# Scatters without a chain, layer 0's experts in two sets of sorted tokens, layer 1's tile weights by ScalarE's queue and its gate rows through DRAM

## The chip, the cores and the metric

The kernel runs on one core of a Trainium2 chip. The time is the device time of one execution in microseconds (us); of several runs the median is taken. Engines are named as the profile names them: PE (TensorE; PEld is its weight load), DVE (VectorE), ACT (ScalarE), POOL (GpSimd), SP (SyncE, which only issues DMAs). A queue is the row of DMAs that one of SP, ACT and POOL issues in its own order of instructions.

## The reference

Two transformer layers on x of 8 batches x 256 tokens x 128 channels, in float32. Every layer modulates with six vectors for each batch, made from a condition c:

```python
mod = (_silu(L0_c) @ L0_wmod).reshape(L0_c.shape[0], 6, 1, -1)
sa, ca, ga, sb, cb, gb = (mod[:, 0], mod[:, 1], mod[:, 2], mod[:, 3], mod[:, 4], mod[:, 5])
...
h = _layernorm(x, axis=-1) * (1 + ca) + sa
x = x + ga * _L0_attn_ref(h, ...)
h = _layernorm(x, axis=-1) * (1 + cb) + sb
x = x + gb * _L0_ffn_ref(h, ...)
```

Layer 1 has the same form with its own parts. Both attentions are causal with 16 heads, of 8 channels in layer 0 and of 64 in layer 1. Layer 0's FFN is a shared expert (128 to 512 to 128, GELU) plus the best 2 of 8 experts of that size for each token, weighted by the router's softmax, divided by the sum of the two. Layer 1's FFN is the token itself, a shared gated expert (128 to 64 to 128, SiLU) and the best 2 of 16 such experts, weighted by a sigmoid router's two values, divided by their sum.

## The kernel before

**Tiling.** The 2048 tokens are 8 batches, 4 windows of 512 (two batches each) and 16 token tiles of 128. The residual x stays in SBUF, one tensor for each window. Transposed, modulated activations h (channels on the partitions) feed the matmuls.

**Order.** The program is written in units, but a scheduler puts each engine's instructions in their final order when the kernel is built, by the tiles that they read and write and by its own estimates of time. So the order of one engine is fixed before the run, and an instruction waits for everything that stands ahead of it on its engine. Tiles come from pools with a fixed number of buffers; a new tile waits until the buffer's earlier user is done. PSUM is used by four names: ps_a with 3 buffers, ps_b with 2, ps_c and the fourth with 1.

**Attention** of both layers runs through `pipelined`: for each unit (a batch and a group of heads) scores, exp on ACT, causal select on POOL (L788), values, and between them `also0` or `also1`, which take one step of a list of further work (layer norms, routing, combining) at each call.

**Sorted experts.** The class `Sorted` (z0, L992, for layer 0 and z1, L993, for layer 1's windows 0 to 2) sends each token to its two experts. `place` finds each token's row within its expert's region (matmul rk, L870; counts pre and seen on POOL, L867) and scatters the rows of one window by 8 indirect DMAs on POOL (L882; one 128-token tile and one choice each, 64 KB) into a DRAM tensor xs that has been cleared. All write to the same tensor, so each waits until the one before has landed. `tables`, called once all windows are placed, makes from the counts the rows and the expert of each tile beyond the first 128 tokens of an expert, and where each token's results will lie (cnt, then some 30 small DVE operations). `load_rows` (L967) loads a tile's 128 rows through SP with a row number read from a register, `load_weights` (L971) its weights through POOL by an indirect DMA (514 KB for layer 0, 128 KB for layer 1), `gather` (L979) brings 128 tokens' results back from the DRAM tensor ys, two indirect DMAs on POOL for each token tile.

**Layer 0's FFN** has 39 tiles: 8 first ones with resident weights wst, then up to 31 more. For each: transpose xT (L1226), hidden hp and GELU hst, projection yt (L1247), a copy to ysb, a store to ys by SP (L1252). Before the tiles stand the last window's routing and, between its parts, the shared expert over the 4 windows (hp L1177, ysh L1190, and the gates' transpose gp with its copy gT, which multiplies the experts' biases). Layer 1 begins with the gathers (L979) of batches 0 to 3, each window's combine (L1347), layer norm 1a (xn1a L739, transposes nt1a L748) and the projections.

**Layer 1's FFN** has 40 tiles in 10 groups of 4 for windows 0 to 2, 16 first ones and 24 more; each group's results leave by one store from ACT's queue, after one copy on DVE and one on ACT (L1582). The last window is not sorted: it runs over 8 pairs of experts and the shared one (g L1596, u L1598, a, of L1617), and its gates are spread over each pair's 128 rows by a copy gm on POOL (L1605) and four transposes gp on PE (L1608), read from PSUM in

```python
nc.vector.tensor_tensor(a, a, gp.rearrange("p a m -> p (a m)"), ALU.mult)
```

(L1609). Then come the gathers of windows 0 to 2, tc (L1643, L1646), the additions to x, and the output's DMAs.

## Time and profile before

| | us |
|---|---|
| median of 3 runs | 710.91 (707.64 to 711.27) |
| profiled execution | 704.31 |
| its span | 702.6 |
| last batch of layer 0's attention (y) ends | 153.8 |
| first expert tile of layer 0 | 206.1 |
| last yt of layer 0 | 286.7 |
| first matmul of layer 1 (nt1a) | 312.9 |
| last y of layer 1's attention | 591.5 |
| last tile group of layer 1 | 637.1 |
| last gather issued | 675.1 |
| last addition ends, then only the output's DMA | 690.7 |

How to read it: the profile is one execution. Each engine's busy time comes first, then the span in 40 slices of 17.6 us with a digit for the busy tenths. Waits are listed as "who, for whom: us in total, times, longest us". "PEclk" is the clock granted to PE, in tenths of full speed. An "issue" wait is time without a recorded cause. A DMA's price has two parts: the time its issue takes on the queue, and the time until it lands (scatter 0.98 and 2.3 us in the median, xg 0.33 and 3.4, ys by SP 0.33 and 2.9, ys by ACT 2.3 to land).

### The profile page before, as it was taken

To read this page: it belongs to the slowest core of one execution; us is meant where nothing else is said; L and a number is where in the kernel's file an instruction comes from. 1 tells how busy PE (TensorE), PEld (TensorE's weight loads), DVE (VectorE), ACT (ScalarE), POOL (GpSimd) and SP (SyncE) were. 2 spreads that over 40 slices of the span, in tenths; PEclk is the share of its full clock that TensorE was granted. 3 is DMA by queue.
4 is the path that set the end of the run, shared out by engine and by line. 5 is a ranking of instruction groups with operands and counts; after the bars stand their busy time and mean duration, and the time that the engine had idled before them with its cause. 6 is when DMAs were issued, how large, how long until landed. Compare 5 with 4: busy or idle time off the path is not lost. (4 is left out here: it accounts for less than half of the span.)

```text
span 702.6 us, 12856 instructions
## 1 busy us (share of the span) xinstructions
PE 583.3 (83%) x4927; PEld 409.7 (58%) x4927; DVE 338.8 (48%) x994; ACT 245.9 (35%) x435; POOL 341.3 (49%) x493
## 2 busy tenths in 40 slices
PE   3898877866969999319999999999989987889672
PEld 3455443433859999316666666667667756654451
DVE  5358566574412222253146345743554585833561
ACT  2546262615125555204433443344323521222110
POOL 6667457744540444475223332247234754864840
PEclk9999899988989999859999999999999999889886
DMA  8899930011253999221011202030203022662220
GB/s 278 313 407 398 375 139 13 21 51 77 80 189 120 292 331 322 63 52 35 2 43 31 65 1 62 1 77 17 62 8 77 10 68 69 183 199 72 60 57 20
DMA packets 48291, 83.30 MB, mean 119 GB/s; under 512 B 6253, under 2 KB 26765, under 8 KB 47069
## 3 DMA queue, kind: packets, MB, share of 16 engines
q1 hardware_dynamic: 33388, 51.84, 22.6%
q0 software_dynamic: 9552, 27.93, 12.8%
q10 hardware_dynamic: 5280, 2.62, 1.3%
q8 instruction: 41, 0.67, 0.4%
q14 instruction: 30, 0.24, 0.1%
HBM read 51.33 MB, written 31.04 MB: 117 GB/s over the span
## 5 line engine op out<-in xcount | busy, mean ns | idle before, releaser
L788 POOL TENSOR_SCALAR_AFFINE_SELECT pt<-pt 128x256 f32<-128x256 f32 (+1 forms) x176 | 90.8, 545 | 117.6 <-ACT pt L1390 104.5
L882 POOL DMA_INDIRECT xs<-ht,idx x56 | 59.4, 1061 | 79.4 <-DMA xs<-ht,idx 65.3
L971 POOL DMA_INDIRECT wt<-in_wpk_dram,widx x55 | 52.6, 956 | 63.3 <-PE xT L1226 50.7
L1390 ACT ACTIVATE pt<-sc 128x768 f32<-128x768 f32 x64 | 48.9, 808 | 88.2 <-PE sc L1387 88.0
L979 POOL DMA_INDIRECT yg<-ys,yidx x56 | 54.0, 965 | 33.5 <-issue 21.9
L1094 ACT ACTIVATE pt<-sc 128x1024 f32<-128x1024 f32 x48 | 46.8, 1021 | 59.7 <-PE sc L1090 58.6
L1407 PE MATMUL o<-pt,v 128*64 128x256 f32 (+1 forms) x512 | 57.1, 337 | 0.0
L1407 PEld LDWEIGHTS o<-pt,v 128*64 128x64 f32 x512 | 34.1, 137 | 32.1 <-issue 14.7
L1387 PE MATMUL sc<-q,k 64*128 64x256 f32 (+1 forms) x512 | 50.9, 338 | 0.0
L1387 PEld LDWEIGHTS sc<-q,k 64*128 64x128 f32 x512 | 41.8, 188 | 10.3 <-issue 5.9
L1238 ACT ACTIVATE hst<-hp,wt 128x128 f32<-128x128 f32 x124 | 35.4, 368 | 26.8 <-ACT hst L1238 17.7
L592 DVE COPY k<-kp 128x512 f32<-128x512 f32 x29 | 20.0, 689 | 43.8 <-PE kp L1363 41.6
L1251 DVE COPY ysb<-yt 128x128 f32<-128x128 f32 x39 | 11.4, 291 | 56.5 <-PE yt L1247 50.9
L1115 PE MATMUL o<-pt,vm 128*32 128x128 f32 (+1 forms) x512 | 32.3, 350 | 6.9 <-POOL pt L788 6.9
L1363 PE MATMUL qp<-h,wq 128*128 128x256 f32 x128 | 36.8, 410 | 0.8 <-DVE h L752 0.8
L1370 PE MATMUL vp<-wv,h 128*128 128x512 f32 x64 | 35.2, 631 | 1.9 <-DVE k L592 1.6
L1090 PE MATMUL sc<-qm,k 32*128 32x512 f32 x192 | 34.0, 646 | 1.0 <-ACT pt L1094 0.9
L1236 PE MATMUL hp<-xTs,wt 128*128 128x128 f32 x248 | 33.5, 278 | 1.5 <-DMA wt<-in_wpk_dram,widx 0.9
L1363 PE MATMUL kp<-h,wk 128*128 128x256 f32 x128 | 34.3, 392 | 0.0
L592 DVE COPY ou<-o 128x512 f32<-128x512 f32 x29 | 19.9, 686 | 28.0 <-PE o L1407 28.0
L1247 PE MATMUL yt<-wt,hst 128*128 128x128 f32 x248 | 32.6, 275 | 0.0
L1236 PEld LDWEIGHTS hp<-xTs,wt 128*128 128x128 f32 x248 | 30.1, 191 | 3.3 <-issue 1.5
(284 smaller groups left out, 1147.8 us busy)
## 6 DMA issues: line engine op xcount, KB each, us to landing
xs<-zero SPq DMA_DIRECT2D x1, 12288.0 KB
xs<-zero SPq DMA_DIRECT2D x1, 8192.0 KB
rb<-rd SPq DMA_DIRECT2D x14, 512.0 KB, 6.2
wst<-in_wpk_dram SPq DMA_DIRECT2D x8, 514.0 KB, 42.5
mdb<-mrd SPq DMA_DIRECT2D x2, 2048.0 KB
xg<-xs SPq DMA_DIRECT2D x63, 64.0 KB, 3.4
ys<-ysb ACTq DMA_DIRECT2D x10, 256.0 KB, 2.3
ys<-ysb SPq DMA_DIRECT2D x39, 64.0 KB, 2.9
```

The lines of the kernel that those rows point to most:

```text
L592: nc.vector.tensor_copy(dst, src)
L788: nc.gpsimd.affine_select(out=pt, in_=pt, compare_op=ALU.is_ge, fill=0.0, base=0, pattern=[[0, pt.shape[1]], [1, P]], channel_multiplier=-1,)
L882: nc.gpsimd.indirect_dma_start(out=self.xs[:, :], out_offset=bass.IndirectOffsetOnAxis(ap=idx[:, j, k : k + 1], axis=0), in_=tokens[:, j, ...
L971: nc.gpsimd.indirect_dma_start(out=wt, out_offset=None, in_=packed, in_offset=bass.IndirectOffsetOnAxis(ap=self.widx[:, d : d + 1], axis=0),)
L979: nc.gpsimd.indirect_dma_start(out=yg[:, k, :], out_offset=None, in_=self.ys[:, :], in_offset=bass.IndirectOffsetOnAxis(ap=self.yidx[:, j, ...
L1094: nc.scalar.activation(pt[:, bass.ts(half, 2), :], sc, AF.Exp)
L1236: nc.tensor.matmul(out=hp[:, c, :], lhsT=wt[:, bass.ts(c, P)], rhs=xT, start=True, stop=True)
L1238: nc.scalar.activation(hs[:, c, :], hp[:, c, :], AF.Gelu_apprx_tanh, bias=wt[:, WB + c : WB + c + 1])
L1363: nc.tensor.matmul(out=ps_[:, n, :], lhsT=w1[f"w{what}1"][:, bass.ts(2 * part + n, P)], rhs=hb, start=True, stop=True,)
L1387: nc.tensor.matmul(out=sc[:, n, cols], lhsT=k[r, c, bass.ts(kb, P)], rhs=q[r, c, qs], start=True, stop=True)
L1390: nc.scalar.activation(pt, sc[:, :, 0:384], AF.Exp, scale=1.0 / math.sqrt(D1))
L1407: nc.tensor.matmul(out=o[bass.ts(n, D1), m, qs], lhsT=v[:, kb, bass.ts(4 * u + 2 * m + n, D1)], rhs=pts[m][:, n, cols], start=(kb == 0), s ...
```

## The change

1. The scatters of one set are declared free of each other (`apart`): each waits for the clearing only; the last of a set waits for all others, and stands for them towards the reader of xs. This is in the class, so it holds for both layers.
2. Layer 0's tokens are two sets: windows 0 to 2 (31 tiles) and window 3 (15 tiles), 46 tiles in place of 39, with two tensors xs (6 and 2 MB) in place of one (8 MB). The first set's tables are made at the end of the attention. Its tiles are written ahead of the shared expert of windows 1 to 3, which now stands between the sets. The gathers of batches 0 to 3, their combine and layer norm 1a of windows 0 and 1 are called beside the second set's tiles; 16 gathers are left to layer 1.
3. `also0` and `also1` take two steps at a call.
4. Layer 1's extra tiles get their weights by a plain DMA on ACT's queue, from an expert number read into a register of ACT. The groups' second copy goes from ACT to DVE, the stores from ACT's queue to SP's.
5. The last window's gates are transposed once (4 transposes, one copy), stored to DRAM (gd) and read back broadcast over 64 partitions by 4 DMAs of SP into gp in SBUF. `gate_rows()` is called ahead of the first tile group. The copies gm and the 32 transposes are gone.
6. Buffers: hs has one buffer, sums1 is gone (r tiles and r_last), hgb is xn itself; mdb1 keeps its place in the program, but its pool opens after the tiles of both sets.

```diff
+    def apart(self, ins):
+        group = f"scatters{self.tag}"
+        if len(self.scatters) + 1 < 2 * self.ng * self.nt:
+            if self.scatters:
+                tc.declare_no_dep(ins, group=group, reason="different rows")
+                tc.add_manual_dep(ins, self.fill.name, WAIT, reason="rows are cleared first")
+        else:
+            for other in self.scatters:
+                tc.add_manual_dep(ins, other.name, WAIT, reason="stands for all scatters")
+        tc.add_to_no_dep_group(group, ins)
+        self.scatters.append(ins)
...
-    z0 = Sorted(xp, "0", E0, NW, TT, (2 * NT - 2) // P)
+    zs0 = [Sorted(xp, f"0{n}", E0, k, TT, (2 * k * TW - 2) // P) for n, k in enumerate((NW - 1, 1))]
...
         def also0(n):
-            if st0["steps"]:
-                st0["steps"].pop(0)()
+            for step in st0["steps"][:2]:
+                step()
+            del st0["steps"][:2]
...
                     st0["steps"].append(lambda w=w: route0(w, ps_ln))
+                    if w == NW - 2:
+                        st0["steps"].append(lambda: zs0[0].tables(ps_ln, True))
...
-        last = layernorm_steps(NW - 1, md[0], SB, CB, f"0b{NW - 1}", ps_b, make_tokens0)
-        last[0]()
-        hs = shared_hidden(0)
-        last[1]()
+        for step in layernorm_steps(NW - 1, md[0], SB, CB, f"0b{NW - 1}", ps_b, make_tokens0):
+            step()
         route0(NW - 1, ps_b)
-        shared_project(0, hs)
-        z0.tables(ps_b)
+        zs0[1].tables(ps_b, True)
...
+        tiles = [(z, n) for z in zs0 for n in range(E0 + z.nd)]
+        first = E0 + zs0[0].nd
+        shared_project(0, shared_hidden(0))
         for n in range(3):
-            fetch(n)
-        for w in range(1, NW):
-            hs = shared_hidden(w)
-            shared_project(w, hs)
...
+            if n == first:
+                for w in range(1, NW):
+                    shared_project(w, shared_hidden(w))
+            if first < n <= first + 4:
+                gather(n - first - 1, fp0)
+            if n == first + 4:
+                combine(0, fp0)
+                combine(1, fp0)
+                steps = layernorm_steps(0, md[1], SA, CA, "1a0", ps_b)
+                steps.pop(0)()
+            if n == first + 6:
+                steps.pop(0)()
+            if n == first + 8:
+                combine(2, fp0)
+                combine(3, fp0)
+                steps = layernorm_steps(1, md[1], SA, CA, "1a1", ps_b)
+                steps.pop(0)()
+            if n == first + 10:
+                steps.pop(0)()
...
-        for b in range(4):
-            gather(b)
-        for step in after0(0):
-            step()
...
-                    z1.load_weights(wt[:, t, :], i["wpk1"], d)
+                    r = nc.values_load(
+                        z1.widx[0:1, d : d + 1], engines=[mybir.EngineType.Activation], min_val=0,
+                        max_val=(E1 - 1) * P, skip_runtime_bounds_check_because="an expert's number, 128 times",
+                    )
+                    nc.scalar.dma_start(out=wt[:, t, :], in_=i["wpk1"][bass.ds(r, P), :])
...
-            nc.scalar.copy(ysb[:, :, 1, :], y[1])
-            nc.scalar.dma_start(
+            nc.vector.tensor_copy(ysb[:, :, 1, :], y[1])
+            nc.sync.dma_start(
...
+        gp = fp1.tile([P, NP, TW], F32, bufs=1, name="gp")
+        def gate_rows():
+            gT_ps = ps_b([E1, TT, P], "gT1")
+            for j in range(TT):
+                nc.tensor.transpose(gT_ps[:, j, :], gates1[:, j, :], ident)
+            gT = fp1.tile([E1, TT, P], F32, bufs=1, name="gTs1")
+            nc.vector.tensor_copy(gT, gT_ps)
+            gd = dram.tile([NP, 2, TW], F32, name="gd1")
+            nc.sync.dma_start(
+                out=gd.rearrange("p n q -> (p n) q"), in_=gT.rearrange("e j t -> e (j t)")
+            )
+            for half in range(2):
+                p = bass.ts(half, NP // 2)
+                for n in range(2):
+                    nc.sync.dma_start(out=gp[bass.ts(n, I1), p, :], in_=gd[p, n, :].partition_broadcast(I1))
...
             if p < NP:
-                gm = fp1.tile([P, TT, 2, I1], F32, tag="gm", bufs=2, name=f"gm1_{w}_{p}")
-                src = gates1[:, :, 2 * p : 2 * p + 2]
-                nc.gpsimd.tensor_copy(gm, src.unsqueeze(3).to_broadcast([P, TT, 2, I1]))
-                gp = ps_b([P, TT, P], f"gp1_{w}_{p}")
-                for j in range(TT):
-                    nc.tensor.transpose(gp[:, j, :], gm[:, j].rearrange("p a m -> p (a m)"), ident)
-                nc.vector.tensor_tensor(a, a, gp.rearrange("p a m -> p (a m)"), ALU.mult)
+                nc.vector.tensor_tensor(a, a, gp[:, p, :], ALU.mult)
...
+        gate_rows()
         for m in range(3):
             fetch1(m)
         turn1(0)
```

## The prediction

> **What bounds the kernel now.** I read the busy table and the 40 slices first, then the waits, then a table of stages. PE is busy 83% of the span, and in slices 12 to 29 it reads 9: layer 1's attention, which the change hardly touches. What can move lies in the other slices.
>
> ```profile
> PE 583.3 (83%) x4927; PEld 409.7 (58%) x4927; DVE 338.8 (48%) x994; ACT 245.9 (35%) x435; POOL 341.3 (49%) x493
> PE   3898877866969999319999999999989987889672
> PEclk9999899988989999859999999999999999889886
> ```
>
> The stages (start:end, length, then busy us of PE, PEld, DVE, ACT, POOL) show where PE is not busy.
>
> ```profile
> 30.00:154.00 124.00, 102.32 (x1318) 57.52 (x1310) 80.54 (x253) 50.55 (x56) 80.38 (x116) 0.94 0.55 209
> 154.00:206.00 52.00, 39.76 (x211) 28.25 (x211) 18.78 (x74) 17.32 (x23) 27.38 (x30) 0.87 0.32 102
> 206.00:287.00 81.00, 78.57 (x663) 75.88 (x663) 19.52 (x78) 45.42 (x157) 24.42 (x26) 0.98 0.79 257
> 287.00:315.00 28.00, 1.28 (x5) 0.86 (x5) 11.52 (x48) 0.70 (x2) 20.53 (x21) 0.58 0.18 47
> 315.00:590.00 275.00, 264.22 (x2171) 183.58 (x2172) 136.90 (x319) 103.78 (x149) 109.55 (x190) 0.99 0.16 37
> 590.00:640.00 50.00, 40.35 (x326) 28.50 (x324) 27.08 (x63) 11.58 (x26) 30.93 (x32) 0.86 0.60 172
> 640.00:702.60 62.60, 39.49 (x160) 23.46 (x158) 29.06 (x55) 5.96 (x10) 30.17 (x32) 0.80 0.16 44
> ```
>
> PE idles 22 us in layer 0's attention, 12 in its routing, 27 between the layers, 11 in layer 1's attention, 33 in the last two stages, 12 of which are the output's DMA after the last addition. The waits (who, for whom, total us, times, longest) say for what.
>
> ```profile
> POOL xs L882 <- DMA xs<-ht,idx: 65.3, 38, 5.1
> PE nt1a L748 <- DVE xn1a L739: 26.3, 1, 26.3
> POOL yg L979 <- issue: 21.9, 51, 8.1
> PEld o L1115 <- POOL pt L788: 10.2, 8, 3.7
> PE rk L870 <- DVE m L862: 8.8, 6, 2.5
> ```
>
> L882 is the chained scatters; behind them on POOL stand the causal selects (L788) that layer 0's values wait for. The 26.3 is one wait: the last expert tile is stored, 12 to 13 gathers must land, window 0 is combined and normalized, and only then has PE layer 1's first matmul. The end is a chain of gathers: after the tiles (yq_9 ends at 637.1) the first of 24 gathers issues at 640.9, the last lands at 677.6, the last window's output is added by 690.7.
>
> ```profile
> POOL yg L979 2%; PE of L1617 1%; DMA yg<-ys,yidx 1%; PE g L1596 1%; PE u L1598 1%; POOL x L1625 0%; DVE a L1609 0%; PE gp L1608 0%; POOL wt L971 0%; DVE tf L1623 0%; DVE tc L1646 0%; DVE x L1627 0%; POOL gm L1605 0%; DVE tc L1643 0%; DVE x L1647 0%
> ```
>
> **What the skill says.** "DMA: Bandwidth & Descriptors", the section on the anatomy of a GpSimd-path DMA: about 2.0 us fixed, most of it the receipt of the last write, plus bytes over 436 GB/s; 64 KB gives 2.15 us. The trace agrees: a scatter issues in 0.98 us and lands 2.3 us later, so a chained one costs 3.3 us and more, an unchained one its issue. Same page, "Issuing engines are not separate DMA queues": another queue saves sequencer time only, so layer 1's weight loads on ACT's queue free POOL and buy no bandwidth. No run here shows that yet. Same page, "Two DMAs through the same engine are not ordered": the second must wait for the first's semaphore, so gate rows through DRAM cost two landings in turn. "TensorE: Matmul & The Clock Gate", Part 1: an idle window of some 3.4 us halves PE's clock. Here PE's granted clock is 0.58 between the layers and 0.87 in the routing stage; after stalls of even 2 us matmuls took twice their time for about 2 us.
>
> **The change, part by part.** Times are on the profiled execution (704.31 us, span 702.6), which lies 6.6 us under the median of 710.91; I carry the difference over.
>
> *A. Scatters apart, layer 0's attention.* Eight scatters take 8 x 1.25 = 10 us (issue 0.98 plus about 0.3 to the next) instead of 8 x 3.3 to 5. In the changed order they sit where PE has 13 us of other work before it needs the next select. The stalls on selects of 1.14, 2.15 and 3.24 us go; of the rank waits about half of 8.8, and one to two us of half-clock work after each. Gain 9 (bounds 3 and 12). Against it: window 0 to 2's table (some 30 small DVE operations of 0.3, 9 us) now stands on DVE ahead of the last batch's reciprocal; I take 1.5 (0 to 4). Layer 0's attention ends at about 146 instead of 153.75: -7.5.
>
> *B. Tiles before window 3 is routed.* Before, 206.06 - 153.75 = 52 us lie between, of which shared windows 1 to 3 took 25 as cover, 4.03 were a wait for a POOL operation behind scatters and 6.00 a wait for xg behind 48 us of scatters. Now the router of window 3 has no shared window beside it (6.5 us of PE idle, at nothing before because hidden), but the 10 us of waits go: tiles start 25 us after attention, 171.
>
> *C. Set 1* is 31 tiles, not 39: the first 8 took 17.3 us, the others 2.04 each: 17.3 + 23 x 2.04 = 64. End 235.
>
> *D. Between the sets* the moved shared windows (25 us) should hide the gathers. But the static order of DVE puts the copy gT_2 behind the combine of gather 13, and gT_3 behind gather 15 and window 0's normalization; PE has the transposes of tiles 2 to 4 of set 2 behind these copies, as two PSUM buffers serve both. The gathers start when ys_30 has landed (235 + 0.3 + 2.9), gather n lands 1.25(n-1) + 2.6 later, with one 1.27 us addition between: the 15th 21 us after the start, at 260, gT_3 at 261.5. PE has 13.5 us of work and is there at 248.5. New stall: 13 (6 if the gathers start earlier than I think, 14 at most), with PE cold behind it, 1 us. Then 11.5 us of shared work and 15 tiles (27 us, 1.8 each, most from resident weights): layer 1's first matmul at about 301.5, not 314.87. The 7 extra tiles are in this: 13 us of PE, and 7 x 642 KB beside it.
>
> *E. Into layer 1.* Before, the first select was at 331.04 and the first value matmul at 337.0. Now 16 gathers (20 us) stand on POOL between the last store's landing (about 303) and the first select: select at 326, values at 328. PE has 22 us of projections and scores, which fill 301.5 to 324. Gain -9. In the same attention scatters and selects meet again. Windows 0 and 1's blocks have 20 us of cover; window 2's last seven (9 to 11 us) stand before a select for which PE has 6.2 us of work: stall 4 (0 to 5). Attention ends at about 586.5, not 591.5: -5.
>
> *F. Last stage.* Taken away: 24 weight issues on POOL (0.96 each, beside other work), 8 gm copies (5 us among the gathers), 32 transposes (8.7 us) on PE. Added: 24 loads on ACT, each with a register load like xg's on SP (0.94 us per load there). Two of these come ahead of the last rstd1b and seven ahead of the routing exp, which on the clock of before starts at 603.6 instead of 598.2 (bounds of the delay 0 and 9). PE has the gate transpose gT ahead of the first tile's; it needs the whole routing chain on DVE (ready at 613.3 before, with POOL's loads beside it; now about 608 on that clock), so tiles begin at 609 instead of 597.7. Loads run ahead meanwhile, so groups then go at PE's pace (31.7 us busy) and at SP's, which carries gd, four gp reads and the ys stores as well: last group 644 instead of 637.1, first gather +6.6. Given back: the gm copies, the gate transposes, and fewer products left behind the last gather, -5. Sum +1.5 (bounds -3 and +7).
>
> Stores by SP instead of ACT: 0.33 against 0.4 us of issue, landing 2.9 against 2.3; no more than 0.6, at the last group only. The second ysb copy on DVE, hgb in xn, r in tiles: no cover lost, nothing. mdb1's 2 MB now stands in SP's queue ahead of set 2's first store; it waits for gT_3 at latest, which is over by then.
>
> *Sum.* Entry of layer 1 -9, window 2's block +4, last stage +1.5: -3.5. So 700.8 for the profiled execution, 707.5 on the median's scale: -0.5%, just what a measurement of this kernel can tell from no change.
>
> **The rivals.** *Faster by much*: the copies in D are not late (the gathers overtake PE's work, or PE's 25 us really cover them) and F's gT costs little since weights bound that stage. Then D gives back 10, F 2 and the block 2: 707.5 - 14 = about 693, and up to 702 if a third comes true. For it: the slices show 54 us of poor PE use between 154 and 315 that the shared windows could fill. Against: the static order of DVE names the gathers ahead of the copies.
>
> *Slower*: head of line in the last stage. PE's gT ahead of xT_0 turns ACT's late exp into a wait of the whole tile stage. From the point where the loads behind it no longer catch up (exp over 6 us late), the 24 gathers, which are the tail chain, start that much later: +10 there, and A worth only 3 (+6): 707.5 + 13 to 16, about 721. For it: ACT has no 3 us of slack between rstd1b at 593.2 and the exp at 598.2. Against: PE had 6 us of idle in 598 to 636 that absorb part.
>
> *No effect*: since the gathers before layer 1's first select stay 16 in number, E's gate on POOL could eat all: +4, 711. It is counted in the middle case.
>
> **Chances.** Middle (702 to 714, forecast 707.5): 0.42. Faster rival (692 to 702): 0.28. Slower rival (714 to 728): 0.30. Four fifths lie in 694 to 722. Faster by over 0.5% (below 707.4): 0.28 + 0.19 = 0.47; within 0.5% (to 714.5): 0.23; slower: 0.30.
>
> **What would show it.** A: waits of scatters on scatters vanish, PE's wait for pt L788 under 3 us, attention ends at 146 to 150. B, C: first xT near 171, last yt of set 1 near 235. D: one PE wait of over 8 us at the transposes of set 2, released by DVE. E: select near 326, values near 328. F: a PE wait of some 11 us for gT, with ACT's loads ahead of the exp; last tile group near 639. Wrong would make me: no wait in D (then faster), a long wait for xg behind the chain to DRAM in F, or set 1 slowed by the second clearing's and shared weights' traffic.

## The result and the profile after

The changed kernel takes 734.61 us in the median (731.78 to 737.06, 4 runs) against 710.7 us (707.64 to 711.27, 4 runs): 1.034 times as long [1.030, 1.039]. Forecast were 707.5 us and a range of 694 to 722. The profiled execution takes 734.42 us, its span is 732.6 us, 30.0 us above that of before. (The medians differ by 23.9; the other 6 us are there because the profiled execution of before, 704.31 us, lies that far under its median.)

The runs below were made on several chips: on some the kernel before takes about 709 us (the faster level), on others about 726 (the slower level), and a ratio is always to runs of before on the same chip. The runs of `one0` and `no_apart1` fell into a lower and an upper group: times and ratios given for them are of the lower, their profiles of the upper.

First the busy table and the slices of after (same columns as before).

```profile
PE 602.6 (82%) x5019; PEld 425.0 (58%) x5019; DVE 349.5 (48%) x1045; ACT 254.4 (35%) x456; POOL 310.7 (42%) x462
PE   3998767675999965996999998999899876569774
PEclk9999989897899996999799999999999979679899
```

PE has more to do (19 us, the 7 tiles more among it), POOL less. The hole between the layers, which read 3 1, now reads 6 5 and comes two slices sooner. But slices 4 to 9, layer 0's attention for the most part, read 8 7 6 7 6 7 instead of 8 8 7 7 8 6, and the last ten 9 8 7 6 5 6 9 7 7 4. The stages of after (start:end, length, busy us of PE, PEld, DVE, ACT, POOL, then granted clock, DMA share, GB/s):

```profile
30.00:154.00 124.00, 96.66 (x1200) 53.64 (x1199) 78.76 (x230) 51.12 (x57) 75.78 (x109) 0.90 0.55 209
154.00:206.00 52.00, 41.44 (x328) 32.34 (x328) 27.83 (x134) 18.50 (x43) 27.32 (x34) 0.80 0.37 126
260.00:287.00 27.00, 13.78 (x69) 10.23 (x68) 13.05 (x52) 7.19 (x9) 15.45 (x16) 0.75 0.16 46
315.00:340.00 25.00, 21.57 (x123) 16.10 (x124) 10.51 (x36) 7.65 (x22) 12.37 (x13) 1.00 0.25 79
590.00:640.00 50.00, 30.72 (x247) 24.31 (x244) 23.92 (x62) 7.73 (x11) 15.52 (x18) 0.80 0.23 66
```

In the 124 us of layer 0's attention PE did 102.3 us of work before and does 96.7 now, at a lower clock: the attention, which should have become shorter, became longer. The hole between the layers (1.28 us busy of 28) has moved to 260:287, where half of the time is idle. The waits of after, those that answer to the ones shown of before:

```profile
PE rk L872 <- DVE m L864: 20.6, 7, 4.7
PE xT L1270 <- DVE gT L1234: 13.2, 2, 9.0
PE nt0b L749 <- DVE xn0b L740: 13.0, 3, 6.4
```

The 65.3 us of scatters waiting for scatters are gone, as is the 26.3 us wait for xn1a, and PE no longer waits for a select in layer 0. In their place stand three waits of PE for DVE: for the rank matmuls (8.8 us before), for layer norm 0b, and between the sets. The last chain ends as before it did, over the last gathers, products and additions.

A ledger by stage, from the times of the tiles in the two traces and the forecast's own:

| stage | before | after | change | forecast |
|---|---|---|---|---|
| start to the last y of layer 0's attention | 153.8 | 167.0 | +13.3 | -7.5 |
| to layer 1's first qp | 161.1 | 156.7 | -4.4 | -5.9 |
| to the last y of layer 1's attention | 276.6 | 294.9 | +18.3 | +8.4 |
| to the last tile group yq_9 | 45.6 | 60.1 | +14.5 | +6.9 |
| to the last addition | 53.6 | 48.8 | -4.8 | -5.4 |
| to the end of the span | 11.9 | 5.1 | -6.8 | 0 |
| sum | 702.6 | 732.6 | +30.0 | -3.5 |

Two rows are right, three are wrong, all to one side. Of the 33.5 us between forecast and profile, 21 lie in layer 0's attention and 10 in layer 1's. The last three rows together came to +2.9 us, against +1.5.

The last row was not forecast, and it is not the output's DMA, as the table ahead of the prediction has it. In the trace of before the output's last bytes land at 694.8; what ends last is a closing step of POOL (696.1 to 701.7). In after POOL has taken that step by 720.2, ahead of the last addition, the output lands at 730.1, and the span ends 2.5 us later. The runs below divide by the gate rows: with gate rows through DRAM this row is 4.8 to 5.3 us, with the whole last stage of before 11.5 to 12.2, in old_gates 8.5.

### The profile page after: what moved, and what is told of

Read it like the earlier page. It is cut to its first block, busy times and chain, and to the rows that moved or that the text cites. A ratio compares the mean times of both kernels' runs of the same rounds, so it can differ in the third digit from the quotient of the medians.

```text
span 732.6 us, 13218 instructions
## 1 busy us (share of the span) xinstructions
PE 602.6 (82%) x5019; PEld 425.0 (58%) x5019; DVE 349.5 (48%) x1045; ACT 254.4 (35%) x456; POOL 310.7 (42%) x462
## 3 DMA queue, kind: packets, MB, share of 16 engines
q1 hardware_dynamic: 41820, 57.51, 24.5%
q0 software_dynamic: 8256, 24.26, 10.1%
## 5 line engine op out<-in xcount | busy, mean ns | idle before, releaser
L789 POOL TENSOR_SCALAR_AFFINE_SELECT pt<-pt 128x256 f32<-128x256 f32 (+1 forms) x176 | 89.1, 535 | 155.4 <-ACT pt L1431 131.5
L884 POOL DMA_INDIRECT xs<-ht,idx x56 | 60.1, 1073 | 27.5 <-issue 16.5
L997 POOL DMA_INDIRECT yg<-ys,yidx x56 | 53.4, 953 | 21.2 <-issue 14.2
L1448 PE MATMUL o<-pt,v 128*64 128x128 f32 (+1 forms) x512 | 52.9, 341 | 5.3 <-POOL pt L789 5.3
L1428 PE MATMUL sc<-q,k 64*128 64x256 f32 (+1 forms) x512 | 57.3, 350 | 0.0
L1428 PEld LDWEIGHTS sc<-q,k 64*128 64x128 f32 x512 | 44.7, 194 | 16.3 <-issue 11.5
L989 POOL DMA_INDIRECT wt<-in_wpk_dram,widx x30 | 28.3, 944 | 53.0 <-PE xT L1270 49.8
L1295 DVE COPY ysb<-yt 128x128 f32<-128x128 f32 x46 | 13.4, 292 | 60.1 <-PE yt L1291 58.4
L595 ACT COPY v<-vp 128x512 f32<-128x512 f32 x29 | 17.0, 586 | 49.7 <-PE vp L1411 39.0
L1136 PE MATMUL o<-pt,oh 128*32 128x128 f32 (+1 forms) x512 | 32.7, 354 | 0.0
L1111 PE MATMUL sc<-qm,k 32*128 32x512 f32 x192 | 31.3, 665 | 0.4 <-ACT pt L1115 0.3
```

The lines of the kernel that those rows point to most:

```text
L789: nc.gpsimd.affine_select(out=pt, in_=pt, compare_op=ALU.is_ge, fill=0.0, base=0, pattern=[[0, pt.shape[1]], [1, P]], channel_multiplier=-1,)
L884: self.apart(nc.gpsimd.indirect_dma_start(out=self.xs[:, :], out_offset=bass.IndirectOffsetOnAxis(ap=idx[:, j, k : k + 1], axis=0), in_=to ...
L997: nc.gpsimd.indirect_dma_start(out=yg[:, k, :], out_offset=None, in_=self.ys[:, :], in_offset=bass.IndirectOffsetOnAxis(ap=self.yidx[:, j, ...
L1136: nc.tensor.matmul(out=o[bass.ts(g, 32), what, q], lhsT=lhsT, rhs=rhs, start=(u == 0 and what == 0 and n == 0), stop=(u == 2 and n == 3), ...
L1428: nc.tensor.matmul(out=sc[:, n, cols], lhsT=k[r, c, bass.ts(kb, P)], rhs=q[r, c, qs], start=True, stop=True)
L1448: nc.tensor.matmul(out=o[bass.ts(n, D1), m, qs], lhsT=v[:, kb, bass.ts(4 * u + 2 * m + n, D1)], rhs=pts[m][:, n, cols], start=(kb == 0), s ...
```

## The experiments

The theory after the result: (1) in layer 0 two steps at a call (A) bring layer norm and rank matmuls to PE before DVE has their inputs; (2) scatters without a chain form blocks of ten microseconds on POOL, and what stands behind the block pays; (3) in layer 1's entry the gathers and the combine stand ahead of selects and copies; (4) in the last stage the weights on ACT's queue and the gate rows hold the tiles. The rival to each: the step is harmless, and the time comes from the pieces that it meets. Below, an attention ends with its last y matmul, the entry of layer 1 is the time from its first qp to its first y, and yq_9 is the last tile group of layer 1.

### Steps of the windows: one at a call

**one0**, layer 0 takes one step at a call again, and what is left follows the loop:

```diff
-            for step in st0["steps"][:2]:
-                step()
-            del st0["steps"][:2]
+            if st0["steps"]:
+                st0["steps"].pop(0)()
...
+        for step in st0["steps"]:
+            step()
         finish0(B - 1)
```

> The changed kernel with one step at a call again in layer 0's attention (also0); steps left over run after its last unit. Theory (head of line): in the changed kernel PE waits 13.0 us for xn0b and 10.8 us for the rank's m in layer 0's attention, because two steps at a call bring the transposes and the rank matmuls forward on PE to a place that DVE has not reached. With one step those waits fall under 6 us together, the last y of layer 0's attention comes at about 152 to 156 us instead of 167, and the time falls by 10 to 13 us, to about 722. Rival (what costs is the second set: 7 more tiles, more traffic): the attention ends earlier by no more than 3 us and the time stays at 732 to 736. Rival 2: the wait returns as a later start of the tiles, since window 2's table is late: attention ends at 155, the first tile's transpose stays at 183.

Measured: 719.85 and 723.62 us, 1.018 [1.009, 1.026]. Layer 0's attention ends at 154.2, 12.8 us sooner than in after, and layer 1's last y at 608.7 against 618.6. (In this profile yq_9 comes 71 us behind the last y, against 60 in after, so its end shows nothing of the gain.) What two steps do is seen in a stretch of after's timeline (start us, length us, engine, line, operation):

```profile
89.36 0.96 POOL L884 DMA_INDIRECT xs<-ht,idx  x1 [0.30 <-issue]
90.34 1.22 POOL L789 TENSOR_SCALAR_AFFINE_SELECT pt<-pt 128x512 f32<-128x512 f32 x2
90.78 6.14 DVE L784 SCALAR_TENSOR_TENSOR good<-r,good 128x256 f32<-128x256 f32 x1
91.54 1.84 POOL L1086 TENSOR_SCALAR qm<-q,jm 128x256 f32<-128x256 f32 x4
93.34 3.30 POOL L789 TENSOR_SCALAR_AFFINE_SELECT pt<-pt 128x512 f32<-128x512 f32 x4
96.96 0.42 DVE L785 SCALAR_TENSOR_TENSOR good<-r,good 128x256 f32<-128x256 f32 x1
100.96 1.16 PE L749 MATMUL nt0b<-ident,xn0b 128*128 128x128 f32 x4 [6.36 <-DVE xn0b L740]
```

Read it from the top. At 90.3 the block of eight scatters is over, and POOL works off what has piled up: ten operations without a gap, to 96.6. DVE's operation `good`, which takes 0.41 us at 75 us in the same trace, starts near the beginning of this row and ends just behind it, 6.14 us later. Layer norm's xn0b stands behind `good` on DVE, and PE, which now has nt0b next in its order, stands idle for 6.36 us. The same happens at 131 us (6.03 and 5.22). "SBUF — State Buffer", section "Who interferes with whom", says that a DVE instruction with two SBUF inputs contends with a GpSimd instruction that reads SBUF. `good` has two inputs, and selects and qm read SBUF. The page speaks of the length of one instruction; here `good` does not get in between ten of them. That this is the cause is read from the overlap; no run measured it alone. In one0 `good` takes 0.41 us beside the same blocks, since it comes elsewhere, and PE waits 5.2 us for rank matmuls instead of 10.8.

**two_steps**, before with nothing but two steps at a call, in both layers (the lines above with the signs turned). The scatters are chained.

> The kernel before with two steps at a call in both attentions, nothing else. Theory: this alone makes layer 0's attention 8 to 13 us longer (PE waits for xn0b and m of some 20 us in place of 8), ratio 1.010 to 1.018. Rival: the waits in the changed kernel came from the scatters' new places and not from the steps: ratio within 0.995 to 1.005.

Measured: 711.98 us, 1.007 [1.004, 1.011], attention of layer 0 ends at 162.9 against 154.8 in the run of before beside it (before_again). The first line is PE's wait for the rank matmuls in two_steps, the second that in before_again, both for 30:168.

```profile
PE rk L870 <- DVE m L862: 10.4, 3, 3.9
```

```profile
PE rk L870 <- DVE m L862: 5.1, 3, 2.2
```

So 8 us at the attention's end belong to the two steps alone, 5 of them in the rank waits; 4 of them are left at layer 1's last y (596.8 against 592.8; the entry takes 60.4 against 59.9). The `good` half needs the blocks as well: `good` takes at most 0.96 us here, and nt0b waits only 1.8 us.

**one1**, the same edit in `also1`.

> The changed kernel with one step at a call again in layer 1's attention (also1) alone. Theory: the waits at the entry of layer 1 (5.7 us for a copy of q on DVE that stands behind the combine of gathered rows) come from the combine's place, which two steps at a call bring forward by a call; with one step the first y of layer 1 comes 3 to 8 us earlier after the first qp, and the time falls by 3 to 8 us, to about 729. Rival: the combine stands ahead of the same copies either way, since it waits for the same gathers: no change (733 to 736).

Measured: 738.41 us, 1.041 [1.035, 1.048], and the entry takes 71.8 us (72.1 in after): no gain. The rival holds in layer 1.

### Scatters apart, layer by layer

**apart_l0** is before with the change's `clear` and `apart`, switched off for layer 1:

```diff
-                    nc.gpsimd.indirect_dma_start(
+                    self.apart(nc.gpsimd.indirect_dma_start(
...
+        def apart(self, ins):
+            if self.tag != "0":
+                return
```

> The kernel before with layer 0's scatters apart, layer 1's chained as before. The run with both apart was 1.7% slower than before. Theory A (blocks of eight hold POOL for 10 us): the loss is in layer 1, where the third block makes PE wait 5.2 us for a select; with layer 0 alone the first tile's wait for xg (6.0 us) and the wait for pre (4.0) are gone, and the time is the same or 1% faster (0.985 to 1.00). Theory B (PE's granted clock falls in layer 0's attention, 0.86 in that run against 0.94): it falls again with layer 0 alone, attention ends 8 us or more later than in the control, ratio 1.005 to 1.015.

Measured: 692.6 us (690.42 to 694.0), 0.978 [0.971, 0.986]. Attention ends at 150.8 (154.8 in before_again below), the first xT follows at 191.8 (203.0), layer 1's first qp at 299.6 (313.8); 14 us are left at layer 1's last y (578.8 against 592.8) and 12 at the end of the span. This is the fastest version of all, at the faster level. Layer 0's part of step A works there, and its larger half lies where B had put it: the routing stage, from the attention's end to the first xT, is 41.0 us long instead of 48.1.

**apart_l1**, the same for layer 1 only (`"1"` in the test). The instructions stand in the order of before on PE and DVE.

> The kernel before with layer 1's scatters apart, layer 0's chained. Theory S (layer 1's blocks of eight are the loss): a block holds POOL for 10 us while selects are due; PE waits 5 us at the third block, ACT's exps wait for buffers at the others, and layer 1's attention takes 8 to 15 us longer than the control's 219 us (first y to last y); ratio 1.008 to 1.02. Theory T (the two sets are the loss): only the third block's 5 us, ratio 1.003 to 1.008.

Measured: 740.32 us, 1.023 [1.016, 1.029]. From first to last y it takes 234.4 us (220.7 in a profile of before at the same level, before_control2 below). A block of its timeline, the first two scatters and the last:

```profile
467.78 1.03 POOL L884 DMA_INDIRECT xs<-ht,idx  x1 [1.99 <-DVE idx L881]
469.12 0.98 POOL L884 DMA_INDIRECT xs<-ht,idx  x1 [0.30 <-issue]
...
476.75 0.96 POOL L884 DMA_INDIRECT xs<-ht,idx  x1 [0.30 <-issue]
477.73 0.78 POOL L789 TENSOR_SCALAR_AFFINE_SELECT pt<-pt 128x256 f32<-128x256 f32 x2
```

Ten microseconds pass without a select. Its waits of PE in 340:622 name one of these blocks and something more:

```profile
PE vp L1388 <- ACT q L595: 7.5, 3, 4.7
PE sum L1433 <- POOL pt L789: 5.5, 1, 5.5
```

Against 0.3 and 1.7 us in before_control2. That is 11 of the 14 us. The 5.5 is window 2's block, which the forecast had as 4. The 7.5, a wait for copies on ACT, is missing from after, on a chip of the faster level: it belongs to the slower level. Its longest part is a copy of q that starts at 479.26, when the block is over, though its matmuls ended at 474.31; apart_only shows more of this.

**apart_only**, both layers, on the slower level of times.

> The kernel before with the scatters apart (both layers), nothing else. Theory: 38 waits of scatters on scatters go, the causal selects of layer 0 are not late, PE's 6.9 us of waiting for them fall under 2, the 6.0 us wait for the first xg and the 4.0 us wait for pre go: attention ends 4 to 7 us earlier, the tiles start 8 to 12 us earlier, and the time is 698 to 704, 1 to 2% under before. Rival: blocks of eight scatters stop POOL for 10 us each just where PE needs a select, so the stalls stay (time 707 to 712), or layer 1's third block adds 5 us as it does in the changed kernel.

Measured: 740.48 us, 1.017 [1.010, 1.025]. Layer 1 as in apart_l1 (234.0 us). But layer 0's attention ended at 168.4, not 151: on this chip the blocks cost time. **best** shows it again, and there the chip's own before is beside it (161.5): with the order of apart_l0 on every engine in this stretch, attention ends at 167.3. First apart_l0, then best, at the first block:

```profile
83.58 1.06 PE L1133 MATMUL o<-pt,oh 128*32 128x128 f32 x32
84.71 1.76 DVE L1143 RECIPROCAL r<-o 128x256 f32<-128x256 f32 x1 [1.41 <-PE o L1133]
85.81 1.94 ACT L1112 ACTIVATE pt<-sc 128x1024 f32<-128x1024 f32 x2 [1.99 <-PE sc L1108]
91.06 0.96 POOL L884 DMA_INDIRECT xs<-ht,idx  x1 [0.30 <-issue]
93.04 2.09 PE L1108 MATMUL sc<-qm,k 32*128 32x512 f32 x8 [3.49 <-POOL qm L1083]
```

```profile
86.14 0.41 PE L1133 MATMUL o<-pt,oh 128*32 128x128 f32 x3 [0.30 <-issue]
91.01 0.96 POOL L884 DMA_INDIRECT xs<-ht,idx  x1 [0.30 <-issue]
93.38 1.76 DVE L1143 RECIPROCAL r<-o 128x256 f32<-128x256 f32 x1 [10.13 <-remote]
93.50 1.94 ACT L1112 ACTIVATE pt<-sc 128x1024 f32<-128x1024 f32 x2 [9.73 <-remote]
95.65 1.22 PE L1156 MATMUL y<-wout,aT 128*128 128x128 f32 x4 [7.62 <-DVE aT L1145]
```

In the first ACT works on within the block, and PE only waits for qm, which stands behind it on POOL. In the second ACT starts nothing for 9.73 us, until the block is over, and PE and DVE stand with it. The two reciprocals say more. r waits for PE's o alone: in apart_l0 it starts 0.07 us behind the end of o, in best 6.8 us behind it. The trace of best has no update of PE's semaphore (the signal that DVE and ACT wait for) between 82.7 and 93.36, though PE ended work at 86.55 and at 87.88. So the work was done and the others learned of it when the block was over; "remote" stands there because no matmul ended near the signal. In each of the ten runs on chips of the slower level some recorded signals of PE come more than 5 us behind the work (up to 14.5 us; up to a tenth of the updates is not on record there), in the ten on chips of the faster level none more than 1.1 us. What delays them is not settled.

**no_apart1**, after with layer 1's scatters chained again (an early `return` in `apart` for tag 1):

> The changed kernel with layer 1's scatters chained again. Theory S: PE's 5.3 us wait for a select in the last batch goes and with it 5 us or more: ratio 1.015 to 1.027 in place of 1.034. Theory T: 5 us at most, ratio 1.027 to 1.034.

Measured: 736.42 and 738.14 us, 1.017 [1.010, 1.025]. From first to last y it takes 216.8 us, against 223.8 and 223.4 in pool_wt and old_gates at the same level. The direction agrees with apart_l1; the ratio rests on two runs.

### Two sets

**sets_only** is after with all scatters chained, one step at a call, and the old last stage (weights by POOL, gm and gp, stores by ACT); what stays of the change are the two sets, the moved calls and the smaller buffers.

> The kernel before with layer 0's two sets alone (the changed kernel with chained scatters, one step at a call, and the last stage as before; the smaller buffers stay). Theory T: 7 more tiles (13 us), a 13 us wait between the sets for copies behind the combines, and 12 us more from the first qp to the first y of layer 1 outweigh the 26.3 us wait that goes: ratio 1.010 to 1.025. Theory S: the sets are level, 0.995 to 1.005.

Measured: 729.41 us, 1.005 [1.002, 1.008]. Layer 1's first qp is at 314.5 and the entry takes 74.2 us. **sets_apart0**, the same with layer 0's scatters apart:

> As the run before, with layer 0's scatters apart. If the parts add, this is 2.2% under it and 0.978 plus what the sets cost. Theory T: 0.988 to 1.003, above the 0.978 of the scatters alone. Rival: with one set the chain of scatters stood ahead of all tiles, with two sets only window 3's block of it does, so most of the 2.2% is gained by either and the second brings little: within 1% of the run with the sets alone.

Measured: 739.46 us, 1.021 [1.015, 1.027]: attention ends at 167.3 instead of 155.6, first qp is at 328.3. On this chip too the blocks cost 12 us in layer 0, and they are not won back in the routing stage: the first tile's hp comes 25.7 us behind the attention, and 27.3 us with chained scatters, as the first set does not wait for the last window's.

### The entry of layer 1

**comb_late** calls after0 one batch later, so that the combine should stand behind the copies.

```diff
-            if u == 0 and b % 2 == 0 and b + 4 < B:
+            if u == 0 and b % 2 == 1 and b + 3 < B:
-                st1["steps"] += after0(b // 2 + 2)
+                st1["steps"] += after0(b // 2 + 2)
```

> The changed kernel with the combine and layer norm of windows 2 and 3 begun one batch later in layer 1 (four calls later), everything else kept. Theory: the 12 us that layer 1's entry loses (first qp to first y: 72 us against 60 before) are the DVE copies of q, k, v standing behind combines that wait for gathers, and the half clock after; moved, the entry takes 60 to 64 us and the time falls by 8 to 12 us, to about 725. Rival: POOL's 16 gathers ahead of the first causal select set the entry whatever DVE does: under 3 us gained.

Measured: 740.26 us, 1.042 [1.035, 1.049], entry 71.3 us. The scheduler put the combine at the same place again, so this run says nothing on the question.

**hold** has the 16 gathers wait for the selects of batches 1 and 3 instead of standing ahead of the first one.

```diff
+                if "hold" in held:
+                    tc.add_manual_dep(ins, held["hold"].name, WAIT, reason="after the first selects")
...
-            if u == 0 and b + 4 < B and b % 2 == 0:
-                gather(b + 4, ap1)
-                gather(b + 5, ap1)
+            if u == 0 and b in (1, 3):
+                held["hold"] = held["select"]
+                gather(b + 3, ap1)
+                gather(b + 4, ap1)
+                del held["hold"]
```

> The changed kernel with layer 1's last 16 gathers made to wait for causal selects of its batches 1 and 3 (a dependency on POOL's own queue) and their combines behind them. In the run with the combine one batch later the scheduler had put it in the same place again, so that run did not test it. Theory: the entry of layer 1 is 12 us longer (first qp to first y 72 us, before 60) because 16 gathers stand on POOL ahead of the first select, and the combines, with the gathers' landings, ahead of DVE's copies of q; held, it takes 60 to 63 us, PE's 5.7 us wait for a copy of q goes, and the time falls by 7 to 12 us, to about 725. Rival: the gathers cost the same later, as a block ahead of batch 1's and 3's selects: under 3 us gained.

Measured: 760.77 us, 1.047 [1.039, 1.055]. Beside old_gates, on the same chip, the first value matmul comes 21.2 us behind qp, not 33.5, and the first y after 66.3 us, not 72.0. So the gathers ahead of the selects set the place of the values, and about 6 us of the entry. But from first to last y it then takes 232.6 us, not 223.4: they cost more in the middle of the attention than at its start. The rival held.

### The last stage

**ffn_only** is before with the change's last stage alone: weights on ACT's queue, stores by SP, gate rows through DRAM ahead of the tiles, no gm and gp.

> The kernel before with the last stage of the change alone: layer 1's tile weights by ACT's queue, stores by SP, gate rows through DRAM, and the buffers that make room for it. Theory: the last tile group ends 57 to 62 us after the last y (45.6 before), of which the dense part gives back 5, so 8 to 10 us slower, ratio 1.010 to 1.015. Rival (that stage lost only because of what the two sets and the scatters did to it): ratio within 0.995 to 1.005. My record's own step F said +1.5 us, 1.002.

Measured: 713.72 us, 1.006 [1.001, 1.010]. From the last y to yq_9 it takes 61.5 us, 44.2 in before_again; from there to the end of the span 53 instead of 66. So the trace has 17 us lost and 12 won, 7 of the 12 behind the last addition. Its waits, PE's, then ACT's:

```profile
PE gT L1600 <- DVE gates L1313: 6.5, 1, 6.5
PE xT L1557 <- DMA xg<-xs: 6.1, 1, 6.1
```

```profile
ACT aq L1572 <- DMA wt<-in_wpk_dram: 12.2, 3, 4.4
ACT L735 <- DMA xg<-xs: 9.8, 1, 9.8
ACT L1299 <- DMA wt<-in_wpk_dram: 4.7, 1, 4.7
```

PE stands for gT, as forecast, then for a row fetch of SP's queue. And ACT's arithmetic waits for DMAs that it does not read: a layer norm's operation (L735) for xg, SiLUs for weights. In the traces the plain DMAs of SP's and ACT's queues use the same eight completion semaphores in turn, and an issue waits until the older transfer with its semaphore has landed. In after a row fetch goes out at 649.34, 0.02 us behind the landing of a read of gp (512 KB) that had its semaphore before it and took 9.6 us to land. On ACT everything behind such an issue waits too. That the semaphores are the reason is read from the traces; no run changed their number.

**gate_late**: `gate_rows()` beside the sixth group instead of ahead of the first.

```diff
-        gate_rows()
         for m in range(3):
             fetch1(m)
...
                 project_tiles(m - 1)
+            if m == 5:
+                gate_rows()
```

> The changed kernel with gate_rows called beside the sixth tile group instead of ahead of the first. Theory (head of line in the last stage): PE's transposes of the gates stand ahead of the first tile's transpose and wait 6.6 us for the routing chain, and SP's gd, gp and their landings stand ahead of tile rows (a 5.4 us wait for xg). Moved, the first tile starts about 8 us earlier after the last y, the last tile group is done 8 to 12 us earlier, and as the gathers follow it, the time falls by 6 to 10 us, to about 726. Rival (the weights by ACT's queue and the stores on SP's set the pace of the tile groups): the first tile starts earlier but the last group ends within 3 us of before, time 732 to 735.

Measured: 732.56 us, 1.033 [1.027, 1.038]. Tiles begin 8.4 us behind the last y instead of 16, yq_9 comes 57.2 us behind it instead of 60.2. Most of the head start is lost again where the gate rows now stand: SP issues the reads of gp at 655.8 to 660.4, they take 12.3 us to land, and between the eighth and the ninth group's yq 12 us pass (658.5, 670.3). The late loads of weights have another cause. The first three lines are from after, the last is from pool_wt, in which POOL issues the loads:

```profile
651.69 0.69 PE L1593 MATMUL xT<-ident,xg 128*128 128x128 f32 x2 [5.37 <-DMA xg<-xs]
660.60 0.93 PE L1617 MATMUL yq<-wt,aq 64*128 64x128 f32 x8
661.17 3.45 ACTq L1578 DMA_DIRECT2D wt<-in_wpk_dram  x4
```

```profile
665.96 0.95 POOL L989 DMA_INDIRECT wt<-in_wpk_dram,widx  x1 [20.34 <-PE yq L1613]
```

Twelve of the 24 loads are out by 630, the others come only from 661 on. The tile wt has three buffers of four loads each, so the 13th load waits until yq has read the first of them, on either queue (and in before: yq ends at 617.1, the load goes out at 617.4). What is late is that yq, behind the row fetch that PE waits 5.37 us for.

**pool_wt**, weights by POOL again, and **old_gates**, gm and gp again, each on after:

> The changed kernel with layer 1's tile weights by POOL's indirect DMAs again, all else kept. Theory (a compute engine's queue in order): in the changed kernel 12 of the 24 loads leave ACT by 630 us, the other 12 stand behind the SiLU of the sixth group and leave at 661 to 673, so the last groups' weights come late; besides, ACT itself waits 4.4 us on a weight landing ahead of the routing exp. With POOL the last tile group ends 47 to 52 us after the last y of layer 1's attention instead of 60, and the time falls by 6 to 10 us, to about 726. Rival (SP's queue, now with gd, gp and the stores, is what holds the groups): last group within 3 us of 60, time 731 to 735.

> The changed kernel with the gate rows as before (copies gm on POOL, 32 transposes), all else kept, ACT's weight loads among them. Theory: the first tile starts about 7 us after the last y instead of 16; what the tile groups win by it is given up again to the ACT queue and to SP, as in the run with gate_rows moved (last group 57 us after the last y), and the last window's products cost 7 us of PE more: time 730 to 736, no change. Rival (the gates through DRAM are the cost of the last stage): time falls by 8 us or more, to 726.

Measured: 747.14 us, 1.027 [1.020, 1.035], and 745.11 us, 1.025 [1.016, 1.033]. To yq_9 they take 67.1 and 52.6 us. Both are of the slower level, where before itself takes 52.8 (before_control2). So with the old gates and the weights still on ACT's queue the stage is as long as in before, and with the weights on POOL again it is not: at this level the gate rows ahead of the tiles are the loss up to yq_9. PE's wait for a row fetch ahead of the sixth group is in after, ffn_only and pool_wt (5.4, 6.1 and 6.2 us), and in neither old_gates nor gate_late (none over 1.7). At the faster level neither run was made.

### Controls and the best version

**before_again** and **before_control2** are before, unchanged, for their profiles.

> The kernel before itself, as a control on the chip of the next three: the chip of the run with the scatters apart gave the kernel before 728 us, so its stages need a profile of the same chip beside them. Every theory expects a ratio of 1.00 (within 0.5%), layer 0's attention to end at about 154 us and layer 1's entry (first qp to first y) to take 60 us.

> The kernel before again, for its stages on the chip of the run above. If the entry of layer 1 (first qp to first y) is bound to the chip it is 70 us on a chip where this kernel takes 726 us, and 60 us where it takes 709; layer 0's attention ends at 154 to 157 us on either. Ratio 1.00.

Measured: 708.55 us, 0.998 [0.995, 1.001], and 726.22 us, 1.001 [0.997, 1.004]. The same program in the same order takes 17 us longer, and its two profiles differ by 25 us (spans of 702.8 and 727.8): 10.1 in the entry of layer 1 (59.9 and 70.0), 8.6 from the last y to yq_9, 6.7 in layer 0's attention. A copy of v in the entry, first of before_again, then of before_control2:

```profile
317.32 1.76 PE L1370 MATMUL vp<-wv,h 128*128 128x512 f32 x2
319.11 0.69 DVE L592 COPY v<-vp 128x512 f32<-128x512 f32 x1 [2.06 <-PE vp L1370]
```

```profile
322.79 1.13 PE L1370 MATMUL vp<-wv,h 128*128 128x512 f32 x2
330.49 0.69 DVE L592 COPY v<-vp 128x512 f32<-128x512 f32 x1 [7.88 <-issue]
```

It is the late start of apart_only again: the copy starts 0.03 us behind its matmuls in the first and 6.6 us behind them in the second, while POOL's gathers go out one after another (the last of that row is issued at 329.5). In the 22 us around the entry's start PE is busy 21.3 us in the first (313:335) and 14.7 in the second (318.6:340.6).

**best** is apart_l0 with the gate rows through DRAM beside the sixth group, weights still by POOL and stores by ACT.

> The kernel before with layer 0's scatters apart and the gate rows through DRAM written beside the sixth tile group; layer 1's weights on POOL, its stores on ACT, its scatters chained, one set in layer 0, one step at a call. Theory: the scatters give 2.2% as before, and the last stage without gm copies and gate transposes gives 3 to 8 us between the last tile group and the end (66 us in the control, 54 in the run with the last stage's part alone), with the tile groups as in the control (44 to 46 us after the last y): ratio 0.968 to 0.975. Rival: the DRAM rows' landings or SP's queue cost the tile groups as much: 0.976 to 0.980. On a chip where the kernel before takes 726 us: if the scatters' gain is bound to the chip, layer 0's attention ends at 165 us or later and the ratio is 0.985 or more.

Measured: 714.59 us (713.66 to 718.95), 0.989 [0.984, 0.994], on a chip of the slower level. From the last y to yq_9 it takes 55.1 us instead of 52.8 in before_control2, from there to the last addition 49.3 instead of 53.5, and to the end of the span 4.8 instead of 11.5: gate rows that stand late give 8.6 us in the last stage. It beats before there; after was not run on this chip, nor apart_l0 (0.978, another chip).

## Why the prediction was wrong

**A, layer 0's attention: the step that failed.** It was put at -7.5: 9 of gain, 1.5 for tables on DVE. It came to +13.3, and these 21 us are most of the miss. The gain from the scatters is real at the faster level (apart_l0: 4 us here and 7 more in the routing stage). What was missing is the change's third item: the working gave two steps at a call no cost at all. They bring PE to nt0b and to the rank matmuls before DVE has their inputs: two_steps loses 8 us at the attention's end by them alone, one0 wins 12.8 by taking them out of the changed kernel. The prediction said that of the rank waits half of 8.8 would go; they went from 8.8 to 20.6. It had asked which selects stand behind a block of scatters, and not what DVE does while POOL works off its backlog.

**B, C, D: right.** Tiles were forecast 25 us behind the attention; the first tile's hp begins 24.0 us behind it (its xT goes ahead, at 16.6). The first set was put at 64 us and takes 62.7. The stall between the sets was put at 13, on copies of gT behind the combine, and is 13.2:

```profile
277.13 0.48 PE L1270 MATMUL xT<-ident,xg 128*128 128x128 f32 x1 [9.01 <-DVE gT L1234]
281.83 0.69 PE L1270 MATMUL xT<-ident,xg 128*128 128x128 f32 x2 [4.22 <-DVE gT L1234]
```

From the set's last yt (253.8) to qp it takes 69.9 us against 66.5. Where an engine's static order was walked through, the numbers came within 4 us.

**E, into layer 1: failed, by 8 us in the entry.** The select was put 24.5 us behind qp and came 23.6 behind it. But the value matmul, forecast 2 us behind the select, came 10 behind it, 33.9 us behind qp and not 26.5; the first y came 72.1 us behind qp, 59.7 in before. After's timeline names what PE waited for:

```profile
346.39 0.94 POOL L997 DMA_INDIRECT yg<-ys,yidx  x1 [0.30 <-issue]
347.34 1.74 POOL L789 TENSOR_SCALAR_AFFINE_SELECT pt<-pt 128x256 f32<-128x256 f32 x4
349.12 2.08 PE L1411 MATMUL vp<-wv,h 128*128 128x512 f32 x2 [5.68 <-DVE q L593]
```

The copy of q stands on DVE behind the combine's products, each of which waits for its gather, so projections and scores, "22 us that fill" the time, did not: they were as late as the select. This is the same mechanism as in D; there it was priced, here it was not. It is read from the trace, since comb_late did not move the copies, and hold moved gathers and combine together. At the slower level before itself has an entry of 70 us, and sets_only 74, so that the sets cost 4 us there and 12 at the faster level; 10 us of before's entry there are the late starts shown under the controls.

E's second half was close. A stall of 4 at window 2's block was forecast, and 5.3 us came, plus 2.0 behind it; from first to last y the attention took 5.9 us more than before. The 14 us and 2.3% of apart_l1 are of the slower level, and 7 of them are waits that after does not have.

**F, last stage: the total near, by luck.** +1.5 was forecast, +2.9 measured; alone (ffn_only) the item costs 0.6%, about 4 us. PE's wait for gT was expected, and so was what the gates give back (-5.4, measured -4.8). Mis-sized is the term for the tiles: +6.9 to the last group, measured +14.5. The forecast had the groups go at PE's pace behind gT. In the runs the four reads of gp, priced by their issue only, hold SP's row fetches, and PE waits for one of them. Against that stand 6.8 us at the end of the span, which the forecast put at nothing: two misses of one size cancel.

**The rivals.** The slower one (721 us) put +10 into the last stage, where +2.9 came, and A's gain as 3; that A could be a loss was in no case. "No effect" had seen that E's gain could go.

**The sum does not close.** Alone, layer 0's scatters give -2.2%, layer 1's +2.3%, two steps +0.7%, the sets +0.5%, the last stage +0.6%: +1.9%, against +3.4%. Two parts of the rest can be named: `good` beside the block needs both two steps and scatters apart, and the gain of 7 us that apart_l0 has in the routing stage is one that the sets take for themselves, as sets_only and sets_apart0 show. But layer 1's scatters and the sets were measured at the slower level, where layer 0's scatters cost time and layer 1's cost more, so the sum is no exact account.

## What to carry to other kernels

A wait on an in-order queue can be what lets the queue's other work through: chained scatters left gaps in which selects ran, and unchained ones made blocks of ten microseconds, good where nothing needed POOL (layer 0, at the faster level) and bad where something did (layer 1). A call that merely comes earlier is a move of every instruction in it, so walk the order of the engine that receives it, and of those that feed it. Six edits in one change hid one that was worth 2% by itself at the faster level: measure the parts alone, and each beside its own chip's before. A total that comes out near can hide two misses: compare stage by stage.

## What the runs showed of the hardware that was not expected

- The same program takes 709 us on some chips and 726 on others, with the same order of instructions; of the 25 us between two profiles 10 lie in the entry of layer 1, where POOL issues gathers back to back, 8.6 between the last y and yq_9, 6.7 in layer 0's attention.
- On chips of the slower level PE's finished work reaches DVE and ACT late while POOL issues indirect DMAs one after another: r starts 6.8 us behind o in best (0.07 in apart_l0), the copy of v 6.6 us behind vp in before_control2 (0.03 in before_again). Why is open.
- One DVE operation of 0.41 us took 6.14 and 6.03 us beside an unbroken row of POOL operations (after, at 90.8 and 131.0).
- Indirect DMAs issue every 1.25 to 1.27 us when nothing holds them (0.96 and a pause of 0.30), for scatters and gathers alike.
- Plain DMAs of SP's and ACT's queues wait for each other through eight completion semaphores that both use: a row fetch went out 0.02 us behind the landing of a 512 KB read issued 9.6 us earlier (after, at 649.34).
